# The differences of x on GpSimd instead of VectorE, with new places for every operation in a two-layer graph network

## The chip, the cores and the metric

The kernel runs on one core of one Trainium2 chip. A core has five engines that run side by side, each through its own queue in order: TensorE (PE, matrix products into PSUM), VectorE (DVE), ScalarE (ACT), GpSimd (POOL), and SyncE (SP), which here issues all the transfers. The metric is the device time of one execution in microseconds (us); the time of the kernel before is the median of three runs.

## The reference

The input is 64 independent graphs of 256 nodes, x of shape 64 x 256 x 256 (float32), and an adjacency matrix of integers for each graph. Two layers follow each other.

```
# layer 0, per graph: 8 heads of 32, four relations r, masks from the adjacency
q, k = x Wq + bq, x Wk + bk
attn = softmax(q k^T / sqrt(32))
out  = sum over r of (attn * (adj == r)) (x Wv[r] + bv[r])
x    = LN(x + out Wo + bo);  x = LN(x + gelu(x W1 + b1) W2 + b2)
# layer 1, per graph: two graph attentions, softmax over axis 1 (the columns' nodes)
for (W, a) in two layers:
    Wh = h W;  e = leaky_relu(Wh a1 + (Wh a2)^T)
    h  = softmax(where(adj > 0, e, -9e15), axis=1) Wh
x = LN(x + h);  x = LN(x + relu(x w_ff1 + b_ff1) w_ff2 + b_ff2)
```

Everything is float32. LN is a layer norm over the last axis.

## The kernel before

**One graph.** A graph is some 225 small operations, each a Python function that issues one or a few instructions for a whole graph (or a half or a head of it). Their short names are used throughout this text:

- load brings in x (xin, already cut into 32x32 squares) and the adjacency (adi). xT transposes x on VectorE. cast and jT make the transposed adjacency (adT) by a transfer. mask0 to mask3 compare it with the four relations, mask4 makes the mask of layer 1 (all on GpSimd).
- qk0 and qk1 are the products for q and k (half the heads each), qkc0 and qkc1 their copies out of PSUM. s0 and s1 are the scores. For each half m and each head h of it: max, exp, rec, nrm (the softmax; VectorE and ScalarE in turns), eT (transposition of the squares on VectorE), eW and eR (a write to HBM and a read from it, which finish the transposition), ec (a copy into PSUM on ScalarE), pm (three masks times the weights, VectorE), pl (the fourth mask, GpSimd). po0 and po1 are the products with the values, oT0 and oT1 their copies.
- The values of the four relations are computed with seven block products in place of eight, in the manner of Strassen and Winograd: vp1 to vp7 on TensorE. Four of them read differences of blocks of x, which xS (x_sums, L453) computes into the tile xs: t1 = a21 - a11, t2 = a22 - t1, t3 = a22 - a21, t4 = a12 - t2. The sums afterwards (va1 to va9 and the first copy vc1) put the values together; vb1 and vb0 add the bias on GpSimd.
- wo, ya: output product and residual. y and yb load and prepare the residual. st, rt, nb, ln with a number from 1 to 4: the four layer norms (VectorE, GpSimd, GpSimd, ScalarE); lg and lb: gain and shift on GpSimd.
- The two feed-forward parts have the prefixes a and b: T, W, R (transposition by way of HBM), u0 to u3 (products), x0 to x3 (activation, Gelu for a, Relu for b), S1 to S4 (differences on GpSimd for a second seven-product scheme), d1 to d7 (its products), e (sums out of PSUM), g and r (residual on GpSimd).
- Layer 1: hT, hW, hR (transposition), ga0, ga1, gac (first product and its copy), ip, z, zm, zx, ze, zd with A or B (masked softmax), h10 and h11, h1c (first attention and copy), h2, h2a (second attention, residual), store.

**The order.** There is no scheduler at run time. PLACES (L28 to L67) gives each operation a place in time, PERIOD is 60. Graph g's operation n stands at g x 60 + PLACES[n]; a sort over all graphs gives one list, and each engine's queue is that list cut down to its own operations (plan, near the end of the kernel). So in the steady part some six graphs are in work, each in another stage, and an instruction whose input is late holds up all that stands behind it on its engine. The values of the places are used for nothing but the order: the chip goes as fast as the waits allow. The loads of the weights (LOAD_PLACE, LOAD_STEP) and their preparation (V_PLACE, FFA_PLACE, GAT_PLACE, FFB_PLACE) are put into the same list.

**Buffers that tie the engines together.** All products but the scores and two banks of the feed-forward parts share two PSUM buffers (pool ps_mm, tag mm, two buffers). A product can start only when the product two before it in that pool has been copied or added out of PSUM. The copies pe of the attention weights share one PSUM buffer, so ec and pm take turns.

**Table loads.** ScalarE's functions come in sets. Between Exp and Gelu the compiler puts a table load ahead of the activation; the other functions used here need none. In the order before, the four Gelu activations ax0 to ax3 stand together between zeA and exp03, both Exp.

Of the kernel before, what the change touches and what calls it, by code (L numbers as in the profile page):

```python
# [14 lines left out]
ALU = mybir.AluOpType  # L15
# [10 lines left out]

PERIOD = 60.0
PLACES = {  # L28
    "load": 23.357, "xT": 44.608, "cast": 52.922, "jT": 64.605, "mask0": 69.219, "qk0": 72.09,
    "qkc0": 73.299, "mask1": 76.86, "s0": 78.011, "max02": 87.686, "exp02": 89.264, "qk1": 89.326,  # L30
    "max00": 91.141, "qkc1": 92.707, "exp00": 96.206, "rec02": 99.233, "max03": 99.873, "max01": 100.286,
    "mask2": 100.655, "rec00": 100.829, "nrm02": 101.294, "eT02": 101.781, "nrm00": 102.264, "xS": 102.642,
    "eT00": 102.765, "mask3": 102.981, "exp03": 104.45, "exp01": 105.68, "eW02": 108.309, "rec03": 109.52,
    "vp1": 110.158, "rec01": 110.803, "y": 111.209, "vc1": 113.257, "vp6": 114.571, "s1": 115.506,
    "va6": 115.853, "vp2": 116.039, "eR02": 119.674, "nrm01": 120.359, "max10": 120.437, "va1": 120.827,
    "yb": 121.298, "eW00": 123.019, "exp10": 123.155, "max11": 124.031, "nrm03": 124.245, "rec10": 125.086,
    "nrm10": 125.786, "max13": 129.917, "eR00": 129.963, "exp11": 130.688, "vp7": 131.698, "eT01": 131.873,
    "exp13": 132.201, "va7": 132.519, "vb1": 132.554, "eT10": 133.02, "max12": 133.458, "pl00": 133.78,
    "exp12": 134.344, "vp5": 135.541, "eT03": 136.074, "va9": 137.432, "va5": 137.492, "vp4": 138.406,
    "va4": 138.429, "eW03": 139.955, "ec02": 139.991, "eW01": 140.081, "pm02": 140.771, "eR01": 142.073,  # L40
    "rec12": 143.085, "pl02": 143.665, "rec11": 144.369, "rec13": 144.684, "vp3": 145.914, "ec01": 146.17,
    "nrm13": 147.545, "pm01": 149.231, "va3": 149.974, "nrm11": 150.098, "pl01": 150.355, "ec00": 151.68,
    "eR03": 151.833, "nrm12": 153.205, "mask4": 154.895, "eT13": 154.901, "pm00": 156.208, "ec03": 156.841,
    "vb0": 157.326, "eW10": 158.121, "pl03": 159.226, "eT11": 159.823, "pm03": 159.89, "eW13": 159.97,
    "eW11": 161.977, "po0": 162.822, "eR11": 162.889, "ec11": 163.67, "oT0": 164.697, "eR10": 165.613,
    "eR13": 166.702, "pm11": 167.743, "ec13": 167.832, "eT12": 167.88, "pl11": 170.085, "pm13": 170.45,
    "pl13": 172.693, "eW12": 172.935, "pl10": 173.109, "ec10": 174.083, "eR12": 178.038, "pm10": 178.658,
    "ec12": 179.982, "pm12": 181.436, "pl12": 183.147, "po1": 190.604, "oT1": 190.634, "wo": 195.515,
    "ya": 196.954, "st1": 198.358, "rt1": 200.264, "nb1": 202.568, "ln1": 205.212, "aT": 205.925,
    "aW": 214.402, "aR": 215.033, "au0": 217.723, "ag": 219.066, "ax0": 219.075, "au1": 220.077,  # L50
    "au2": 220.423, "ax1": 220.498, "au3": 221.942, "ax2": 222.429, "ax3": 223.227, "aS1": 224.059,
    "aS3": 226.672, "aS2": 228.949, "ad1": 229.288, "ad5": 232.772, "ad7": 233.221, "ar": 236.067,
    "ad6": 237.512, "aS4": 241.549, "ad2": 244.054, "ae5": 244.725, "ad3": 244.935, "ad4": 246.881,
    "ae1": 248.098, "ae6": 248.952, "ae": 249.383, "ae7": 250.355, "st2": 254.869, "rt2": 255.472,
    "nb2": 255.506, "ln2": 255.669, "lg2": 259.788, "lb2": 259.86, "hT": 261.844, "hW": 265.63,
    "hR": 271.783, "ga0": 272.609, "gac0": 274.207, "ga1": 274.252, "gac1": 274.962, "ipA": 275.589,
    "zA": 275.992, "zmA": 277.16, "zxA": 278.103, "zeA": 278.374, "zdA": 283.105, "h10": 283.502,
    "h11": 286.253, "h1c0": 287.71, "h1c1": 289.589, "ipB": 290.919, "zB": 291.939, "zmB": 292.107,
    "zxB": 294.725, "zeB": 295.859, "zdB": 298.561, "h2": 301.635, "h2a": 303.541, "st3": 304.449,
    "rt3": 304.465, "nb3": 307.95, "ln3": 307.966, "bT": 311.255, "bW": 313.954, "bR": 315.237,  # L60
    "bu0": 319.27, "bx0": 320.506, "bu1": 320.552, "bu2": 322.215, "bx1": 323.13, "bu3": 323.143,
    "bx2": 325.826, "bg": 326.199, "bx3": 327.872, "bd1": 328.16, "bS1": 328.916, "br": 329.424,
    "bd5": 330.387, "bS2": 331.057, "bS4": 331.173, "bS3": 331.831, "bd2": 334.692, "be5": 334.871,
    "bd3": 337.158, "bd4": 337.445, "bd6": 337.996, "be": 338.193, "be1": 338.799, "bd7": 340.197,
    "be6": 343.454, "be7": 346.517, "st4": 346.806, "rt4": 355.06, "nb4": 361.434, "ln4": 362.111,
    "lg4": 364.143, "lb4": 369.218, "store": 370.908,
}  # L67
LOAD_PLACE, LOAD_STEP = 62.0, 3.0
V_PLACE, FFA_PLACE, GAT_PLACE, FFB_PLACE = 92.0, 199.0, 202.0, 260.0

# [11 lines left out]
def kernel(  # L84
# [12 lines left out]
    nc = tc.nc  # L97
# [43 lines left out]
    def weight(w, name, mixed=False):  # L141

        k, n = w.shape[0] // P, w.shape[1]
        t = const.tile([P, k, n], F32, name=name)
        if mixed:
            mixed_rows(t, w)
        else:
            loads.append((t, w.rearrange("(k p) n -> p k n", p=P)))
        return t
# [13 lines left out]
    def rowvec(v, n, name):  # L163
        t = const.tile([P, n], F32, name=name)
        loads.append((t, _row(v, n)))
        return t
# [37 lines left out]
    wo, bo_r = weight(Wo, "wo"), rowvec(bo, D, "bo_r")  # L204
# [227 lines left out]
    class Graph:  # L432
# [15 lines left out]
        def x_sums(self):  # L448
            self.xs = fp.tile([P, 4, P], F32, tag="xs", name=f"xs{self.g}", bufs=1)
            (a11, a21), (a12, a22) = ([self.xT[:, k, c * P:(c + 1) * P] for c in range(C)] for k in range(KD))  # L450
            t1, t2, t3, t4 = (self.xs[:, i] for i in range(4))
            for o, t, u in ((t1, a21, a11), (t2, a22, t1), (t3, a22, a21), (t4, a12, t2)):
                nc.vector.tensor_tensor(o, t, u, ALU.subtract)  # L453

        def cast(self):
            self.adb = fp.tile([P, C, N], BF16, tag="adb", name=f"adb{self.g}", bufs=1)
# [355 lines left out]
```

## Time and profile before

| what | value |
|---|---|
| median of three runs | 3677.94 us (3675.18 to 3685.38) |
| the profiled execution, own time | 3687.13 us |
| its span | 3685.0 us |
| TensorE, busy | 3497.9 us |
| GpSimd, busy | 3019.8 us |
| VectorE, busy | 2880.7 us |
| ScalarE, busy | 2628.1 us |
| read from HBM and written to it | 243.42 and 201.33 MB |

The profile is one execution. The span runs from the first to the last instruction that it records. A row of instructions gives the line of the kernel, the engine, the operation, output and input tiles, their shapes and the count, then the busy time in us and the mean of one instruction in ns, then the engine's idle time just before them and what ended most of it. A row of a stretch of time gives its bounds and length, then for TensorE's matmuls, its weight loads, VectorE, ScalarE and GpSimd the busy time and in brackets the instructions, then the granted clock, the mean share of the transfer engines and GB/s. A row of waits gives the engine and the line that waited, what it waited for, the us in total, the number of times and the longest. A row of the chain of waits gives start and length in us, the engine, the tile and the line. A float32 matmul appears as two instructions.

### The profile page before, as it was taken

The page shows a single profiled execution, that of the slowest core. Times are in us where ns is not written, and L with a number is a line of the kernel's source. Part 1 is how long each engine was busy: PE and PEld are TensorE (multiplying, and loading weights), DVE is VectorE, ACT ScalarE, POOL GpSimd, SP SyncE. Part 2 cuts the span into 40 slices and gives each one's busy share as a digit, 9 for nine tenths or more (in the row PEclk, how much of TensorE's full clock was granted, in tenths as well). Part 3 has the DMA queues.
Part 4 walks back from the last instruction along what each step waited for, and adds up shares of the span by engine and source line. Part 5 has one row for each costly group of instructions (what it writes and reads, how often), then busy time and mean ns, then how long its engine had stood idle before and what let it go on. Part 6 is the DMA issues. An engine that isn't in the chain of part 4 may idle for free.

```text
span 3685.0 us, 73450 instructions
## 1 busy us (share of the span) xinstructions
PE 3497.9 (95%) x25816; PEld 2749.5 (75%) x25816; DVE 2880.7 (78%) x5208; ACT 2628.1 (71%) x6981; POOL 3019.8 (82%) x3142
## 2 busy tenths in 40 slices
PE   6799999999999999999999999999999999999995
PEld 3577777777777777777777777777777777777775
DVE  5688888878888888778788788788788888788762
ACT  4577777777777777777777777777777777777752
POOL 4588888888888888888888888888888888888864
PEclk8899999999999999999999999999999999999997
DMA  6344444444444444444444443444444444444420
GB/s 180 111 119 124 135 126 124 133 118 124 137 124 123 134 126 123 131 127 122 132 127 124 134 128 121 133 127 123 128 126 124 132 126 123 134 127 123 126 86 26
DMA packets 809889, 457.97 MB, mean 124 GB/s; under 512 B 334256, under 2 KB 718896, under 8 KB 809520
## 3 DMA queue, kind: packets, MB, share of 16 engines
q1 hardware_dynamic: 809520, 453.27, 42.1%
q8 instruction: 204, 3.34, 0.4%
q14 instruction: 165, 1.35, 0.1%
HBM read 243.42 MB, written 201.33 MB: 121 GB/s over the span
## 4 chain that ended last, share of the span: by engine, by line
PE 62%; DVE 17%; ACT 8%; DMA 6%; issue 3%; POOL 2%; SPq 2%; POOLq 0%; ACTq 0%; DVEq 0%
PE ffb_ps L387 10%; PE v_ps L511 9%; PE po L589 5%; PE ffa_po L422 5%; DVE pm L572 4%; PE ffb_pq L422 4%; PE qk_ps L487 4%; PE ffa_ps L387 4%; DVE eT_sq L306 4%; PE ffb_po L422 4%; PE ffa_pq L422 3%; PE ga_wps L619 3%; PE s L537 3%; DVE nmax L542 3%; PE h_ps L678 2%
## 5 line engine op out<-in xcount | busy, mean ns | idle before, releaser
L572 DVE TENSOR_TENSOR pm<-rel,pe 128x1536 f32<-128x1536 uint8 x512 | 891.4, 1741 | 123.4 <-ACT pe L568 110.7
L577 POOL TENSOR_TENSOR pl<-rell,eT 128x512 f32<-128x512 bf16 x512 | 595.9, 1170 | 15.5 <-DMA eT<-eT_d 15.2
L560 ACT ACTIVATE e<-e,rden 128x256 f32<-128x256 f32 x1024 | 463.0, 503 | 145.3 <-DVE rden L555 145.1
L387 PE MATMUL ffa_ps<-ffa_T,w 128*128 128x256 f32 x2048 | 478.2, 382 | 8.9 <-ACT e L550 3.3
L550 ACT ACTIVATE e<-s,nmax 128x256 f32<-128x256 f32 x1024 | 475.5, 475 | 5.6 <-DVE nmax L542 4.6
L387 PE MATMUL ffb_ps<-ffb_T,f 128*128 128x256 f32 x2048 | 458.0, 382 | 20.9 <-DMA ffb_T<-ffb_T_d 20.8
L387 PEld LDWEIGHTS ffb_ps<-ffb_T,f 128*128 128x128 f32 x2048 | 392.4, 192 | 102.9 <-issue 36.2
L387 PEld LDWEIGHTS ffa_ps<-ffa_T,w 128*128 128x128 f32 x2048 | 377.1, 192 | 55.3 <-ACT e L550 5.3
L589 PE MATMUL po<-pm,v 128*32 128x256 f32 x6144 | 363.7, 384 | 19.9 <-DVE pm L572 6.6
L568 ACT COPY pe<-eT 128x512 f32<-128x512 f32 x512 | 306.9, 599 | 87.0 <-ACT gb_wh L659 48.0
L306 DVE STREAM_TRANSPOSE eT_sq<-e 128x512 f32<-128x512 f32 x512 | 354.2, 692 | 14.9 <-DMA eT_d<-eT_sq 9.8
L542 DVE TENSOR_REDUCE nmax<-s 128x2 f32<-128x512 f32 x512 | 342.9, 670 | 5.8 <-PE s L537 5.8
L395 ACT ACTIVATE ffb_h<-ffb_ps,bf_c 128x256 f32<-128x256 f32 x512 | 212.4, 466 | 183.2 <-PE ffb_ps L387 183.2
L520 DVE TENSOR_TENSOR v<-v,v_ps 128x512 f32<-128x512 f32 x448 | 298.7, 678 | 35.0 <-PE v_ps L511 32.5
L430 DVE TENSOR_TENSOR ffb_res<-ffb_po,ffb_res 128x256 f32<-128x256 f32 (+2 forms) x256 | 130.4, 509 | 240.7 <-PE ffb_po L422 134.5
L589 PEld LDWEIGHTS po<-pm,v 128*32 128x32 f32 x6144 | 206.8, 110 | 149.1 <-issue 18.2
L479 POOL TENSOR_SCALAR rel<-adT 128x512 uint8<-128x512 bf16 x192 | 289.7, 1509 | 18.8 <-DMA adT<-adb 17.6
L528 POOL TENSOR_TENSOR v<-v,bv_r 128x512 f32<-128x512 f32 (+1 forms) x128 | 232.5, 1816 | 71.5 <-DVE v L520 71.5
L410 POOL TENSOR_TENSOR ffa_h<-ffa_h,ffa_h 128x512 f32<-128x512 f32 x64 | 82.0, 1281 | 221.9 <-ACT ffa_h L395 217.5
L395 ACT ACTIVATE ffa_h<-ffa_ps,b_c 128x256 f32<-128x256 f32 x512 | 212.2, 465 | 36.0 <-PE ffa_ps L387 35.0
L364 ACT ACTIVATE ffa_res<-ffa_res,nb_x,rs_x 128x256 f32<-128x256 f32 x256 | 139.9, 593 | 135.5 <-POOL nb_x L359 135.5
L550 ACT ACTIVATION_READ_ACCUMULATOR e<-s,nmax 128x1 f32 x1024 | 211.1, 206 | 0.0
(154 smaller groups left out, 8444.7 us busy)
## 6 DMA issues: line engine op xcount, KB each, us to landing
eT_d<-eT_sq SPq DMA_DIRECT2D x512, 256.0 KB, 3.1
eT<-eT_d SPq DMA_DIRECT2D x512, 256.0 KB, 3.1
xin<-in_x_dram SPq DMA_DIRECT2D x256, 64.0 KB, 2.7
adi<-in_adj_dram SPq DMA_DIRECT2D x64, 256.0 KB, 3.3
y<-in_x_dram SPq DMA_DIRECT2D x64, 256.0 KB, 4.6
ffa_T_d<-ffa_T_sq SPq DMA_DIRECT2D x64, 256.0 KB, 3.5
ffa_T<-ffa_T_d SPq DMA_DIRECT2D x64, 256.0 KB, 2.9
hT_d<-hT_sq SPq DMA_DIRECT2D x64, 256.0 KB, 3.2
```

Source lines behind the costliest of these rows:

```text
L306: nc.vector.transpose(self.sq.rearrange("p a c k y -> p (c k) a y"), src.rearrange("p c (k a x) -> p (c k) a x", k=KD, a=A))
L387: nc.tensor.matmul(p[:, f - f0, :], self.wa[:, k, f * P:(f + 1) * P], self.x.nodes(k), start=(k == 0), stop=(k == KD - 1))
L395: nc.scalar.activation(self.h[half][:, f1 + f, :], self.ps[f0][:, f, :], self.func, bias=self.ba[:, f0 + f:f0 + f + 1])
L422: nc.tensor.matmul(self.p[bank][:, k], a[:, f], seven[self.name[:3]][i][:, f], start=(f == 0), stop=(f == KF // 2 - 1))
L511: nc.tensor.matmul(self.ps["v", i], a, wv_s[i], start=True, stop=True)
L542: nc.vector.tensor_reduce(self.nmax[m, h], self.s4[m][h].rearrange("p (c n) -> p c n", c=C), AX.X, ALU.max, negate=True)
L550: nc.scalar.activation(e[:, ic, :], self.s4[m][h][:, ic * N:(ic + 1) * N], AF.Exp, bias=self.nmax[m, h][:, ic:ic + 1], accum_out=self.den[ ...
L560: nc.scalar.activation(e[:, ic, :], e[:, ic, :], AF.Copy, scale=self.rden[m, h][:, ic:ic + 1])
L568: nc.scalar.copy(self.pe[m, h], self.et[m, h].t.rearrange("p b c k y -> p (b c k y)"))
L572: nc.vector.tensor_tensor(self.pm[m, h], self.rel.rearrange("p r b c k y -> p r (b c k y)"), bc(self.pe[m, h], [P, R - 1, C * N]), ALU.mult)
L577: nc.gpsimd.tensor_tensor(self.pm_l[m, h], self.rel_l.rearrange("p b c k y -> p (b c k y)"), self.et[m, h].t.rearrange("p b c k y -> p (b ...
L589: nc.tensor.matmul(po[hp, :], self.v[m][:, jc, r, hp], w, start=(r == 0 and jc == 0), stop=(r == R - 1 and jc == C - 1))
```

## The change

The four differences of x_sums (L453) are issued by GpSimd instead of VectorE. All places are new: 225 of them and the five constants, so that the order on every engine's queue is another. PERIOD stays 60. The instructions themselves are otherwise the same, tile for tile.

```diff
@@ -26,47 +26,47 @@
 PERIOD = 60.0
 PLACES = {
...
-    "eT00": 102.765, "mask3": 102.981, "exp03": 104.45, "exp01": 105.68, "eW02": 108.309, "rec03": 109.52,
...
-    "vb0": 157.326, "eW10": 158.121, "pl03": 159.226, "eT11": 159.823, "pm03": 159.89, "eW13": 159.97,
-    "eW11": 161.977, "po0": 162.822, "eR11": 162.889, "ec11": 163.67, "oT0": 164.697, "eR10": 165.613,
...
-    "aW": 214.402, "aR": 215.033, "au0": 217.723, "ag": 219.066, "ax0": 219.075, "au1": 220.077,
-    "au2": 220.423, "ax1": 220.498, "au3": 221.942, "ax2": 222.429, "ax3": 223.227, "aS1": 224.059,
...
-    "zA": 275.992, "zmA": 277.16, "zxA": 278.103, "zeA": 278.374, "zdA": 283.105, "h10": 283.502,
-    "h11": 286.253, "h1c0": 287.71, "h1c1": 289.589, "ipB": 290.919, "zB": 291.939, "zmB": 292.107,
...
+    "qkc0": 97.949, "s0": 114.109, "mask1": 114.874, "max02": 120.516, "max01": 124.15, "exp02": 124.943,
...
+    "rec02": 126.88, "nrm02": 128.516, "max00": 137.875, "max03": 138.248, "exp01": 142.049, "xS": 142.083,
+    "eT02": 142.989, "exp00": 144.909, "rec01": 145.054, "qk1": 145.647, "exp03": 145.994, "eW02": 148.03,
...
+    "pl03": 192.932, "pl01": 194.193, "ec03": 194.796, "vb0": 194.872, "pm03": 195.848, "eT10": 196.442,
+    "eR13": 197.184, "eT12": 197.655, "po0": 199.032, "ec11": 199.429, "eW10": 200.338, "oT0": 203.052,
...
+    "aW": 243.237, "aR": 244.635, "au0": 248.422, "au1": 248.889, "ax0": 249.225, "ax1": 250.028,
+    "au2": 253.377, "aS1": 255.511, "ax2": 257.28, "au3": 257.297, "ag": 259.726, "ax3": 259.931,
...
+    "zA": 307.902, "zmA": 307.921, "zxA": 308.379, "zeA": 312.657, "zdA": 315.675, "h10": 324.462,
+    "h11": 325.343, "h1c0": 325.47, "h1c1": 325.478, "ipB": 327.18, "zB": 327.348, "zmB": 328.529,
...
-LOAD_PLACE, LOAD_STEP = 62.0, 3.0
-V_PLACE, FFA_PLACE, GAT_PLACE, FFB_PLACE = 92.0, 199.0, 202.0, 260.0
+LOAD_PLACE, LOAD_STEP = 96.0, 3.0
+V_PLACE, FFA_PLACE, GAT_PLACE, FFB_PLACE = 100.0, 240.0, 290.0, 300.0
@@ -450,7 +450,7 @@
             (a11, a21), (a12, a22) = ([self.xT[:, k, c * P:(c + 1) * P] for c in range(C)] for k in range(KD))
             t1, t2, t3, t4 = (self.xs[:, i] for i in range(4))
             for o, t, u in ((t1, a21, a11), (t2, a22, t1), (t3, a22, a21), (t4, a12, t2)):
-                nc.vector.tensor_tensor(o, t, u, ALU.subtract)
+                nc.gpsimd.tensor_tensor(o, t, u, ALU.subtract)
```

Two places are compared modulo 60, since the graphs follow each other at that distance. Counted from po0, the parts that the prediction speaks of stand like this in ScalarE's queue, around the end of a period:

```
before:  zA, exp00, ec03, zeA, ax0, ax1, nrm02, nrm00, ax2 | zdA, ax3, ec11, exp03, oT0, exp01, h1c0
after:   zA, nrm02, ax0, ax1, zeA, ec03, zdA, ax2 | ec11, ax3, exp01, oT0, exp00, h1c0
```

In the second line zeA, an Exp, stands between ax1 and ax2, both Gelu: the compiled program of the changed kernel has 255 table loads. In TensorE's queue the same stretch is, behind ga1 and ipA:

```
before:  d3, d4 (b), au0, d6, au1, d7, au2, au3 | po0, h10, h11, ad1, vp1, ipB
after:   au0, au1, d6, d2, d3, d4 (b), au2, au3, d7 | po0, h10, h11, qk1, ipB, ad1
```

GpSimd's queue has there, after: vb0, aS1, ag, xS, ar, aS3, aS2, aS4, pl11.

## The prediction

> **What bounds it now.** First the page's busy times, then the stretches of equal length, then TensorE's waits, then the chain of waits over one period.
>
> ```profile
> span 3685.0 us, 73450 instructions
> PE 3497.9 (95%) x25816; PEld 2749.5 (75%) x25816; DVE 2880.7 (78%) x5208; ACT 2628.1 (71%) x6981; POOL 3019.8 (82%) x3142
> ```
>
> ```profile
> 0.00:100.00 100.00, 57.60 (x318) 31.89 (x318) 55.97 (x94) 41.09 (x119) 42.45 (x41) 0.80 0.67 179
> ...
> 1000.00:2000.00 1000.00, 974.70 (x7275) 769.84 (x7274) 810.36 (x1466) 741.68 (x1974) 855.54 (x888) 1.00 0.43 127
> 2000.00:3000.00 1000.00, 974.85 (x7310) 768.88 (x7308) 809.92 (x1475) 741.09 (x1972) 849.74 (x884) 1.00 0.44 128
> ```
>
> In the middle TensorE is busy 97.5% at full clock and GpSimd 85%; the others have room. How long is one period (one graph)? The read of hT happens once per graph:
>
> ```profile
> L327 SPq DMA_DIRECT2D hT<-hT_d x36: 635/637/650, 1045.7 to 2978.8; - x36
> ```
>
> So 1933.1 / 35 = 55.23 us. TensorE's share is 0.9748 x 55.23 = 53.84 us, its idle time 1.39 us. Its waits between 1000 and 3000 us (36.2 periods) say where:
>
> ```profile
> PE h_ps L664 <- ACT oT L595: 31.2, 36, 1.4
> PE ga_wps L619 <- DMA hT<-hT_d: 10.1, 12, 2.7
> PE ffa_ps L387 <- DMA ffa_T<-ffa_T_d: 3.2, 4, 1.6
> ```
>
> Nearly all is one wait, 0.86 us per period, before the second half of h1: its PSUM buffer is released by ScalarE's copy oT0. The chain of waits shows why that copy is late:
>
> ```profile
> 1669.60 1.01 DVE xs L453
> 1671.33 0.62 DVE eT_sq L306
> ...
> 1672.45 0.50 ACT ga_wh L659
> 1672.94 0.72 ACT ffa_h L395 x2
> 1673.67 0.49 ACT pe L568
> 1674.17 1.28 ACT L550
> 1675.84 0.65 ACT e L550 x3
> 1676.80 1.14 PE h_ps L664 x4
> ```
>
> VectorE spends its time on xs ahead of the reciprocal for ScalarE's zdA (ga_wh); zdA holds up ax3 (ffa_h), ec11 (pe), a table load of 1.28 us (L550) and an exponential, and only then comes oT0. So xs is on the path that sets the period. 63 x 55.23 = 3479 us of the span are periods, 206 us are fill and drain.
>
> **What the Trainium skill says.** GPSIMD Engine Reference, section 8 (Key points): GpSimd shares its SBUF interfaces with VectorE, and contends with VectorE's instructions of two SBUF inputs. The trace agrees: the first of the four differences takes 247 to 1106 ns, the later ones 281 to 294 ns. ScalarE: Activation LUTs, What ACT_TABLE_LOAD costs: a load of about 1283 ns plus a drain of about 1380 ns. The trace has 1283 ns, and the activation starts at once behind it (load from 1663.95, next at 1665.25), so I use 1.28 us alone. Perfetto Trace Analysis, Identifying the Most-Contended Engine: matmul busy share is a poor measure of the distance to roofline. I therefore use it only for its complement, the idle gaps, which the waits confirm (1.28 of 1.39 us).
>
> **The change, part by part.**
>
> ```profile
> L453 DVE TENSOR_TENSOR xs<-xT 128x128 f32<-128x128 f32 x128 | 64.6, 505 | 0.0
> L453 DVE TENSOR_TENSOR xs<-xT,xs 128x128 f32<-128x128 f32 x128 | 36.9, 288 | 2.2
> ...
> L528 POOL TENSOR_TENSOR v<-v,bv_r 128x1024 f32<-128x1024 f32 x64 | 151.2, 2363 | 20.0 <-DVE v L520 20.0
> L528 POOL TENSOR_TENSOR v<-v,bv_r 128x512 f32<-128x512 f32 x64 | 81.3, 1270 | 51.5 <-DVE v L520 51.5
> ```
>
> Differences: VectorE loses (64.6 + 36.9) / 64 = 1.59 us per graph. GpSimd gets four of 128x128. The two L528 rows give (2363 - 1270) / 512 = 2.13 ns per column and 0.18 us fixed, so 0.45 us each, 1.8 us per graph (bounds: 1.3 us if the fixed part overlaps, 2.5 us if waits between the dependent ones show). GpSimd goes from 0.853 x 55.23 = 47.1 to 48.9 us of at least 53.84: still under TensorE. Its cover: the differences now stand right after ag, at about 52.5 us behind po0's start, and their first reader vp6 comes about 20 us later. What is behind them (ar, aS3, aS2, aS4, for the ad products) has about 5 us. If GpSimd were late by more than that, TensorE would pay one for one.
>
> Places: TensorE's 43 products per graph are the same, so its 53.84 us stay; only the idle time can move. I laid the new queues beside each other from po0's start, with the durations of the rows, and 0.25 us from a product's end to its reader (oT0 after po0 in the trace: 0.2 to 0.3). The tight places:
>
> h1's second half: after au2 ScalarE has a load 1.28, ax2 0.72, ec11 0.50, ax3 0.72, a load 1.28, exp01 0.92: 5.4 us. TensorE has au3 1.73, bd7 0.89, po0 3.59: 6.2 us. So oT0 starts when po0 ends, takes 0.27 to 0.37, and h10 (0.9 us) covers it, with 0.4 us left. The 0.86 us wait goes. Next late is the product behind h11, qk1, which needs h1c0 behind oT0 and exp00 (0.27 + 0.92 + 0.3 after po0 against 1.8 us of h10 and h11): about nothing left.
>
> Table loads: before, two per graph (L395 and L550). Now zeA (Exp) stands between ax1 and ax2 (Gelu), so there are four: +2.56 us for ScalarE, 0.742 x 55.23 = 41.0 to 43.5 us. One is between zA and ax0: zA, nrm02, load, ax0 end 3.9 us after au0's start; the reader bd2 comes at 1.73 + 1.73 + 0.89 = 4.35: 0.5 us left. The other, ahead of ax2, waits for au2: load and ax2 end 2.1 us behind it, po0 needs the buffer after 2.6 us: 0.5 us left. Without this cover each costs 1.28 us.
>
> Transfers: hT is issued behind lb2's transpose; 3.2 us to land, 3.8 us for the read (medians of the issues). It lands 1.2 us before ga0. For ffa_T, ya, st1, rt1, nb1, ln1 and aT (with GpSimd's lb2 and mask1 ahead of rt1) take 6.8 us from wo's end, the write 3.5, the read 2.9: 13.2 us and some issue time, against 13.6 us of products from wo's end to au0: 0.2 to 0.4 us left, about as before, where it stalled 0.09 us per period. SP passes the store between aW and aR, which is free while aW is in flight. The read eR11 now waits for pl01 at GpSimd's end of period, 1.8 us early for ec11.
>
> V products: vp5 needs va7, which reads vp7: 0.25 + 0.60 against vp2's 0.86, about 0.1 us short; wo after va1 about 0.1 us long.
>
> Sum per period: 0.1 (vp5) + 0.1 (qk1) + 0.2 (ffa_T) + 0.1 for the rest = 0.5 us idle in place of 1.39: period 54.3 us. 63 x 0.93 = 58 us less. Fill and drain: the same products in the same order until graph 2, the deferred loads at the same step, the GAT weights (L269 to L284, 14 us of TensorE and waits from 93.7 to 107.8) later; I take nothing, plus or minus 10 us. The profiled execution took 3687.13 us, 2.1 more than its span and 9.2 more than the median of 3677.94. So 3677.9 - 58 = 3620 us.
>
> **Rivals.** A: TensorE without gaps. The slacks above all hold, 0.1 us idle: 63 x 1.28 = 81 us less, 3597 us. For it: every queue but TensorE's has over 4 us free. Against: several slacks are near zero and transfers vary (the eT writes land in 2.0 to 6.0 us).
>
> B, slower: the table loads. If ScalarE comes to zA or to au2's end late by more than 0.5 us, the load is on TensorE's path, at bd2 and at po0. Both wholly exposed cost 2 x 1.28 us less nothing: idle 0.5 + 2.56 = 3.06 us, 63 x 1.67 = 105 us more, 3783 us; with the half-microsecond slacks still there 2 x 0.78 us, 2.06 us, 63 x 0.67 = 42 us more, 3720 us, which I take. It decides from 1.39 - 0.5 = 0.9 us of exposed load on. For it: ec00, just ahead of zA, waits for pm01 and for eR01's landing. Against: ec00 ends 0.2 us before the ips product.
>
> C, no difference: the wait on oT0 goes, but ffa_T or GpSimd's rt3 (which now stands behind mask0, held until pm12 is done) takes its place with 0.9 us: 1.4 us idle, 3678 us. For it: 0.3 us of slack on a path with two landings. Against: the same path stalled only four times in 36 periods.
>
> That the differences alone don't help is no case of its own: they are on the chain shown.
>
> **How the numbers follow.** Forecast 0.52 (own range 3600 to 3650), A 0.2, C 0.12 (3650 to 3690), B 0.16. Within 0.3% means 3667 to 3689, about what a measurement of this kernel tells from no change. Faster: forecast, A and a little of C, 0.74; same 0.10; slower 0.16. The range takes in A with a fill that is 12 us shorter (3585) and the lower half of B (3700); GpSimd's 1.3 to 2.5 us lies within its slack.
>
> **What would show it.** Right: h_ps waiting for oT near 0; 255 table loads (129 before) of 1283 ns; L453 on POOL at about 0.45 us; VectorE busy 2780, GpSimd 3130, ScalarE 2790 us; hT reads 54.3 us apart; TensorE over 98.5% in the middle. Wrong: pq waiting for ffa_h (L395), ffa_ps waiting for ffa_T in most periods, or any single TensorE wait over 0.9 us per period.

## The result, and the profile after

The changed kernel takes 3574.5 us (median of four runs, 3572.94 to 3575.81); the kernel before, beside it, 3680.6 us. The ratio is 0.9712, with a 95% interval from 0.9695 to 0.9729: 106 us less. The forecast was 3620 us, 58 us less. The direction and the mechanism were right, the size was not: the time fell below the low end of the range.

First the busy times of the changed kernel's page.

```profile
span 3571.2 us, 73514 instructions
PE 3477.1 (97%) x25816; PEld 2704.2 (76%) x25816; DVE 2805.2 (79%) x4952; ACT 2776.8 (78%) x7107; POOL 3117.9 (87%) x3398
```

VectorE, ScalarE and GpSimd stand at 2805, 2777 and 3118 us, where 2780, 2790 and 3130 had been worked out. The stretches of equal length (length, then busy time of TensorE's matmuls, its weight loads, VectorE, ScalarE, GpSimd) say more:

```profile
0.00:100.00 100.00, 59.55 (x332) 35.34 (x333) 59.37 (x96) 48.91 (x135) 47.23 (x51) 0.78 0.72 193
1000.00:2000.00 1000.00, 999.84 (x7493) 782.42 (x7486) 811.85 (x1431) 810.05 (x2075) 910.65 (x990) 1.00 0.45 131
```

In the middle TensorE has no idle time left: 999.84 of 1000 us, against 974.7 before. Its waits between 1000 and 3000 us, the whole list, are one line:

```profile
PE ffa_ps L387 <- DMA ffa_T<-ffa_T_d: 0.2, 1, 0.2
```

The wait for oT is gone, the waits for hT are gone, and nothing has taken their place. The hT reads, once per graph, give the period; first those between 1000 and 3000 us, then all.

```profile
L327 SPq DMA_DIRECT2D hT<-hT_d x38: 645/650/660, 1003.7 to 2987.5; - x38
L327 SPq DMA_DIRECT2D hT<-hT_d x64: 585/648/661, 141.6 to 3509.0; - x64
```

The period is (2987.5 - 1003.7) / 37 = 53.62 us, against 55.23: 1.61 us less. 63 periods give 101.4 us. The span fell by 3685.0 - 3571.2 = 113.8 us; the other 12.4 us are what is left over (fill and drain: span less 63 periods, 205.5 before and 193.1 after). The first hT read comes at 141.6 us in place of 161.2. The medians lie 106 us apart and not 114, because the profiled execution of before was 6.5 us above its median and that of after 1.6 us below.

The chain of waits of the changed kernel over the stretch where before it had run through xs, the table load and oT0 (start, length, engine, tile and line):

```profile
1663.08 3.46 PE ffa_ps L387 x16
...
1667.43 3.59 PE po L589 x64
1671.02 1.94 PE h_ps L664 x8
1672.96 0.73 PE qk_ps L487 x3
```

It is TensorE alone, one product after another: au2 and au3, bd7 (left out here), po0, h10 and h11, qk1. Over the whole execution it holds 95% of the chain. The moved differences and the table loads, by groups of instructions (busy time and mean, then the idle time before them):

```profile
L453 POOL TENSOR_TENSOR xs<-xT 128x128 f32<-128x128 f32 x128 | 59.2, 463 | 0.0
...
L395 ACT ACT_TABLE_LOAD x127 | 162.9, 1283 | 12.5 <-PE ffa_ps L387 12.2
L651 ACT ACT_TABLE_LOAD x65 | 83.4, 1283 | 3.6 <-DVE gb_max L646 2.5
```

The differences take 0.46 us each on GpSimd (the two with xs among their inputs 459 ns), 1.84 us per graph, as estimated (0.45 and 1.8).

### The profile page after: what moved, and what is told of

Its sections match the earlier page's. It is cut to its first block, busy times and chain, and to the rows that moved or that the text cites. A ratio compares the mean times of both kernels' runs of the same rounds, so it can differ in the third digit from the quotient of the medians.

```text
span 3571.2 us, 73514 instructions
## 1 busy us (share of the span) xinstructions
PE 3477.1 (97%) x25816; PEld 2704.2 (76%) x25816; DVE 2805.2 (79%) x4952; ACT 2776.8 (78%) x7107; POOL 3117.9 (87%) x3398
## 3 DMA queue, kind: packets, MB, share of 16 engines
q14 instruction: 167, 1.37, 0.1%
## 4 chain that ended last, share of the span: by engine, by line
PE 95%; DMA 1%; DVE 1%; SPq 1%; POOL 1%; ACT 0%; issue 0%; POOLq 0%; ACTq 0%; DVEq 0%
PE po L589 13%; PE ffa_ps L387 12%; PE ffb_ps L387 12%; PE v_ps L511 11%; PE qk_ps L487 6%; PE ffa_po L422 6%; PE ffb_po L422 6%; PE ffa_pq L422 5%; PE ffb_pq L422 5%; PE s L537 4%; PE h_ps L664 3%; PE h_ps L678 3%; PE ga_wps L619 3%; PE wo_ps L609 3%; SPq L139 1%; PE ga_ips L631 0%
## 5 line engine op out<-in xcount | busy, mean ns | idle before, releaser
L387 PE MATMUL ffa_ps<-ffa_T,w 128*128 128x256 f32 x2048 | 465.9, 381 | 8.3 <-DMA ffa_T<-ffa_T_d 8.2
L589 PE MATMUL po<-pm,v 128*32 128x256 f32 x6144 | 361.6, 384 | 15.7 <-POOL v L528 12.3
L395 ACT ACTIVATE ffb_h<-ffb_ps,bf_c 128x256 f32<-128x256 f32 x512 | 214.6, 470 | 160.6 <-PE ffb_ps L387 154.7
L589 PEld LDWEIGHTS po<-pm,v 128*32 128x32 f32 x6144 | 188.7, 110 | 184.1 <-ACT e L560 46.2
L395 ACT ACTIVATE ffa_h<-ffa_ps,b_c 128x256 f32<-128x256 f32 x512 | 208.5, 475 | 5.5 <-PE ffa_ps L387 3.8
L496 ACT ACTIVATE qT<-qk_ps,bqs_c 128x256 f32<-128x256 f32 x128 | 60.7, 474 | 188.5 <-PE qk_ps L487 188.5
L354 POOL TENSOR_TENSOR rs_x<-rs_x,nhalf 128x2 f32<-128x2 f32 x256 | 184.0, 719 | 21.3
L430 DVE TENSOR_TENSOR ffa_res<-ffa_po,ffa_res 128x256 f32<-128x256 f32 (+2 forms) x256 | 133.4, 521 | 69.9 <-PE ffa_po L422 65.6
```

The source lines that it names most:

```text
L387: nc.tensor.matmul(p[:, f - f0, :], self.wa[:, k, f * P:(f + 1) * P], self.x.nodes(k), start=(k == 0), stop=(k == KD - 1))
L395: nc.scalar.activation(self.h[half][:, f1 + f, :], self.ps[f0][:, f, :], self.func, bias=self.ba[:, f0 + f:f0 + f + 1])
L589: nc.tensor.matmul(po[hp, :], self.v[m][:, jc, r, hp], w, start=(r == 0 and jc == 0), stop=(r == R - 1 and jc == C - 1))
```

## The experiments

The runs stand in three groups, each with its own runs of the kernel before; ratios are compared, not times. In the first group before took 3686.1 us, in the second 3683.7 us, in the third 3684.0 us. Periods are worked out from the hT reads as above.

### One half of the change at a time

The differences alone on GpSimd, with the places of before:

```diff
--- kernel before
-                nc.vector.tensor_tensor(o, t, u, ALU.subtract)
+                nc.gpsimd.tensor_tensor(o, t, u, ALU.subtract)
```

> The kernel before with one line changed: the four differences on GpSimd, all places as before. Theory (VectorE's differences are on the path to oT0): 1.59 us leave VectorE ahead of the reciprocal for zdA, oT0 comes before h11 needs it, so the wait of h_ps on oT (0.86 us per period in the records, some 0.14 us more that the modelled ends hide) goes and the waits on hT and ffa_T stay: 63 x 1.0 = 63 us less, 3617 us (3600 to 3650), h_ps <- oT near 0. Rival (it is the new order that does it, the differences' engine does not matter): within 15 us of the kernel before, 3665 to 3680, h_ps <- oT still 0.8 us per period.

Measured: 3635.3 us, ratio 0.9864 (0.9849 to 0.9879), about 50 us less than before; period 54.34 us. From TensorE's waits of this kernel between 1000 and 3000 us, the largest and what is left of the wait for oT:

```profile
PE ga_wps L619 <- DMA hT<-hT_d: 6.2, 9, 1.8
...
PE h_ps L664 <- ACT oT L595: 0.7, 3, 0.4
```

The wait of h_ps for oT fell from 31.2 us to 0.7. So the reading of the chain before was right: xs on VectorE was what made oT0 late. Taking it away gave 55.23 - 54.34 = 0.89 us per period, about the 0.86 us of that wait. What it does not cure are the waits of ga0, for hT above all.

The places alone, with the differences back on VectorE:

```diff
--- changed kernel
-                nc.gpsimd.tensor_tensor(o, t, u, ALU.subtract)
+                nc.vector.tensor_tensor(o, t, u, ALU.subtract)
```

> The changed kernel with the differences back on VectorE, at the same new place (behind be7, ahead of eT02). Theory (the new places do nearly all by themselves, since VectorE has some 1.6 us to spare there: pm11, the next long one, waits for po0's end anyway): 3575 to 3590, TensorE still without waits. Rival (the differences must leave VectorE): 1 us idle per period comes back, 3620 to 3650.

Measured: 3585.7 us, ratio 0.9727 (0.9711 to 0.9743); period 53.81 us. The places alone bring nearly all of it, though on VectorE the differences now cost twice what they did before:

```profile
L453 DVE TENSOR_TENSOR xs<-xT,xs 128x128 f32<-128x128 f32 x128 | 104.8, 819 | 2.2
```

With the first and third, 102.5 us, that is 3.2 us per graph against 1.59, and TensorE hardly minds: the waits on record are 1.0 us in 2000. The two halves are therefore not two gains to be added (50 and 100 us, together 106): each takes the same wait away by itself, and the new places also take away the waits for hT and most of those for ffa_T. Which of the 225 places do it was tried for one alone, zeA (next experiment); for the others it stays open.

What the differences on GpSimd add to the new places is 0.19 us per period, 12 us by the periods and 6 to 8 us by the ratios (0.9727 against 0.9712 and, in the second group, 0.9706), whose intervals overlap. The trace shows where the 0.19 us lie. First TensorE's and then ScalarE's queue with the places alone, and last the same product (ad2, ffa_pq) in the changed kernel:

```profile
1682.08 1.95 PE L422 MATMUL ffa_po<-w,ffa_h 128*128 128x128 f32 x16
1683.95 1.16 PE L422 MATMUL ffa_pq<-w,ffa_h 128*128 128x128 f32 x8
```

```profile
1681.63 0.59 ACT L568 COPY pe<-eT 128x512 f32<-128x512 f32 x1 [1.01 <-DVE pm L572]
...
1683.06 0.83 ACT L638 ACTIVATE gb_z<-gb_ips,gb_wh 128x256 f32<-128x256 f32 x2
```

```profile
1676.61 1.06 PE L422 MATMUL ffa_pq<-w,ffa_h 128*128 128x128 f32 x8
```

In the changed kernel ad2 starts 0.16 us ahead of the recorded end of the product before it, as products in a row do. With the places alone the lead is 0.08 us, and ad2's first matmul takes 0.38 us in place of 0.28. That is so in each of the 37 periods between 1000 and 3000 us, and 0.08 + 0.10 us is about the difference. ad2 starts there 0.05 us after zB (gb_z) ends on ScalarE; in the changed kernel zB had ended 0.69 us before. ScalarE in turn had waited 1.01 us for VectorE's pm, which stands behind the slow differences. So the differences on VectorE still reach TensorE, by a stop too short to be listed as a wait.

### The two extra table loads

With zeA (Exp) put ahead of ax0 again there is no Exp between Gelus, and 129 loads instead of 255:

```diff
--- changed kernel
-    "zeA": 312.657,
+    "zeA": 309.0,
```

> The changed kernel with zeA moved ahead of ax0 in the order, so that there are two table loads per period instead of four (129 in all). Theory (the two extra loads are covered, and the price of having ax0 and ax1 early): ax0 now waits for zxA and zeA, ends about 1.2 us after bd2 wants its buffer, TensorE waits for it (ffb_pq <- ffa_h): 62 x 1.2 = 75 us more, 3650 us (3620 to 3670), though ScalarE is 2.56 us per period less busy. Rival (the loads cost something): 3574 or less.

Measured: 3678.4 us, ratio 0.9982 (0.9973 to 0.9991). With 126 table loads fewer, 2.5 us less work for ScalarE in every period, the kernel is some 100 us slower than the changed kernel, practically the kernel before. The theory had the direction and the place; its 75 us were too few. ScalarE's queue in this kernel (start, length, then in brackets the idle time ahead and what ended it), and below it TensorE's:

```profile
1646.20 0.51 ACT L651 ACTIVATE ga_z<-ga_z,ga_max 128x256 f32<-128x256 f32 x1 [0.85 <-DVE ga_max L646]
...
1647.31 1.28 ACT L395 ACT_TABLE_LOAD   x1
```

```profile
1646.97 1.05 PE L422 MATMUL ffb_po<-f_t,ffb_t 128*128 128x128 f32 x8
1649.50 1.16 PE L422 MATMUL ffb_pq<-f,ffb_h 128*128 128x128 f32 x8 [1.47 <-ACT ffa_h L395]
```

zeA needs the maximum from VectorE and waits 0.85 us for it; its own two exponentials with their accumulator reads take another 1.1 us; only then come the load and, at 1648.60, ax0, and bd2 waits for the buffer. The wait on record is 51.4 us in 36 periods, 1.43 us each, and the period is 55.31 us, 1.69 more than the changed kernel's. The two extra loads are the price for having zeA where nobody waits for it.

### How much slack ScalarE has at bd2

By the trace of the changed kernel, ScalarE's load and Gelus end about 0.4 us before bd2 needs their buffer:

```profile
1657.73 1.28 ACT L395 ACT_TABLE_LOAD   x1
1659.02 1.57 ACT L395 ACTIVATE ffa_h<-ffa_ps,b_c 128x256 f32<-128x256 f32 x4
...
1666.19 0.84 ACT L395 ACTIVATE ffa_h<-ffa_ps,b_c 128x256 f32<-128x256 f32 x2
```

```profile
1655.89 3.62 PE L387 MATMUL ffa_ps<-ffa_T,w 128*128 128x256 f32 x16
1659.35 1.05 PE L422 MATMUL ffb_po<-f_t,ffb_t 128*128 128x128 f32 x8
1660.24 1.06 PE L422 MATMUL ffb_pq<-f,ffb_h 128*128 128x128 f32 x8
...
1667.36 2.80 PE L589 MATMUL po<-pm,v 128*32 128x256 f32 x48
```

The four Gelu instructions of ax0 and ax1 run from 1659.02 to 1660.59; ax0 is the first two of them, and ends near 1659.85. bd2 starts at 1660.24, so 0.4 us are left. ax2 ends at 1667.03 and po0 starts at 1667.36: 0.3 us. To measure the first slack rather than read it, one or three extra copies of about 0.4 us were put just ahead of that load (range(1) below, and range(3)):

```diff
--- changed kernel, in Ffn.act
+                if f0 == 0 and self.func is AF.Gelu:
+                    for _ in range(1):
+                        nc.scalar.copy(self.h[0][:, 0, :], g1_r)
```

The changed kernel stood beside them:

> The changed kernel itself once more, as the mark for the other three of this group: the same ratio to the kernel before as measured first, 0.971, on a profile with hT reads 53.6 us apart and TensorE above 99.9% in the middle.

> The changed kernel with one more ScalarE copy of 128x256 (about 0.4 us) in each graph, just ahead of the table load of ax0; the copy's result is overwritten. Theory (the place beside bd2 has about 0.4 us of slack, as read from the trace): within 8 us of the changed kernel, TensorE waiting for ffa_h at L422 between 0 and 0.1 us per period. Rival (the slack is an artefact of modelled ends and in truth used up): 0.3 to 0.4 us per period, 19 to 25 us slower.

> As the kernel with one more copy, with three (about 1.2 us). Theory (0.4 us of slack, then one for one): 0.8 us per period, 50 us slower than the changed kernel, nearly all of it as TensorE waiting for ffa_h at L422. Rival (ScalarE's lateness is passed on to other places as well, as with the shortened table loads, where the recorded wait was 1.43 us but the period grew by 1.69): over 1.1 us per period, 70 us or more.

Measured: the changed kernel 3574.1 us, ratio 0.9706 (0.9691 to 0.972), period 53.62 us; one copy 3579.3 us, 0.9719 (0.9702 to 0.9735), period 53.68 us; three copies 3630.0 us, 0.9857 (0.9842 to 0.9872), period 54.52 us. So one copy costs 5 us, at the edge of what can be told (the intervals overlap), and three cost 56 us. By how much they make ScalarE late is best read from ax0: it starts 3.13 us behind au0 in the changed kernel, 3.44 with one copy, 4.31 with three (medians between 1000 and 3000 us). So ax0 is 0.31 and 1.18 us late, and the period 0.06 and 0.90 longer: 0.25 and 0.28 us were covered. The kernel with fewer loads gives a third point: ax0 5.09 us behind au0, 1.96 late, the period 1.69 longer, 0.27 covered. So the slack is 0.25 to 0.28 us, less than the 0.4 read from the trace, and behind it ScalarE's lateness goes one for one into TensorE. No wait is on record with one copy, but bd2's first matmul takes 0.36 us in place of 0.28 in 35 of 37 periods, and in none of the changed kernel's:

```profile
1662.77 1.14 PE L425 MATMUL ffb_pq<-f,ffb_h 128*128 128x128 f32 x8
```

So one copy just uses the slack up. With three copies the waits on record are at the place forecast (L425 and L398 are L422 and L395, three lines further down):

```profile
PE ffb_pq L425 <- ACT ffa_h L398: 25.5, 37, 0.7
```

### What stands right behind TensorE

Part of the computation left out, so that TensorE has less to do:

```diff
--- changed kernel, in the products of the feed-forward parts
-            for f in range(KF // 2):
+            last = KF // 2 - 1 if self.func is AF.Gelu else 1
+            for f in range(last + 1):
...
-                                 start=(f == 0), stop=(f == KF // 2 - 1))
+                                 start=(f == 0), stop=(f == last))
```

> The changed kernel with less TensorE work: each of the seven products of the second feed-forward part sums two of four blocks only, so half of that down product is left out. That takes 28 of its 56 block products, about 3.1 us of TensorE per period. Theory (TensorE alone sets the period): period near 50.5 us, some 195 us less than the changed kernel, 3380 us. Rival (GpSimd at 48.6 us per period, ScalarE's waits and the transfers stand right behind): period 51.5 to 52.5 us, 70 to 130 us less, with new waits of TensorE of 1 to 2 us per period.

Measured: 3506.5 us, ratio 0.9523 (0.9509 to 0.9537), 68 us less than the changed kernel; period 52.52 us. The theory fell. The rival comes close: its waits of 1 to 2 us are there, but the period and the gain lie just outside what it gave (51.5 to 52.5 us, 70 to 130 us). TensorE's largest waits of this kernel between 1000 and 3000 us:

```profile
PE po L590 <- ACT ffa_h L395: 44.9, 38, 1.2
PE ffb_pq L423 <- ACT ffa_h L395: 11.2, 37, 0.3
```

These are the two places with a table load, po0 and bd2, with 1.48 us per period between them. In this order of the queues TensorE leads the next bound by only 53.62 - 52.52 = 1.1 us per period. (The shortened products bd6 and bd7 stand right ahead of bd2 and po0 and are part of what covers the table loads, so this is a bound for this way of shortening TensorE's work, not for every one.)

### The fill

The five constants that place the weights' loads and preparation, set back to where they stood in the kernel before, counted from the new places:

```diff
--- changed kernel
-LOAD_PLACE, LOAD_STEP = 96.0, 3.0
-V_PLACE, FFA_PLACE, GAT_PLACE, FFB_PLACE = 100.0, 240.0, 290.0, 300.0
+LOAD_PLACE, LOAD_STEP = 98.2, 3.0
+V_PLACE, FFA_PLACE, GAT_PLACE, FFB_PLACE = 128.2, 235.2, 238.2, 296.2
```

> The changed kernel with the one-time work (the loads of the weights and the four preparations) put where it stood before, counted from po0: loads from 98.2, V at 128.2, first feed-forward at 235.2, attention weights at 238.2, second at 296.2. Theory (the fill became 20 us shorter because this work stands elsewhere): the first read of hT comes at about 160 us instead of 141.6, 3590 to 3597 us. Rival (the graphs' own new order shortened the fill): the first hT within 5 us of 141.6, 3570 to 3580 us.

Measured: 3580.3 us, ratio 0.9713 (0.9699 to 0.9728), by the ratio not to be told from the changed kernel. The first hT read is at 151.1 us, about half way back to 161.2, but the last one at 3515.1, 3 to 6 us after the changed kernel's (3509.0 and 3511.7 in its two profiles). So the constants account for half of the earlier first read, and most of that doesn't reach the end: neither the theory's 3590 to 3597 us nor the rival's first read came out.

Two tries for a shorter fill, with three constants, and with V_PLACE alone of them:

```diff
--- changed kernel
-LOAD_PLACE, LOAD_STEP = 96.0, 3.0
-V_PLACE, FFA_PLACE, GAT_PLACE, FFB_PLACE = 100.0, 240.0, 290.0, 300.0
+LOAD_PLACE, LOAD_STEP = 96.0, 4.0
+V_PLACE, FFA_PLACE, GAT_PLACE, FFB_PLACE = 139.0, 240.0, 290.0, 310.0
```

> The changed kernel with three constants of the start alone: LOAD_STEP 4.0, V_PLACE 139.0, FFB_PLACE 310.0, so that the weights' preparation stands later in the queues. Theory (the fill is set by waits for weights and by the v products' weights on VectorE, the largest of them po waiting for v, 12.3 us once): first hT read 3 to 8 us earlier than in the changed kernel (141.6 to 143.0 us), ratio to the kernel before 0.968 to 0.970. Rival (the waits at the start stand behind each other, so that one removed gives its time to the next): first hT within 2 us, same ratio, 0.9706.

> The changed kernel with V_PLACE 139.0 alone (the preparation of the v products' weights on VectorE stands behind the first maxima and reciprocals of graph 0). Theory: half of what the three constants give, first hT 1 to 4 us earlier. Rival: no change within 2 us.

Measured: 3575.0 us, ratio 0.9701 (0.9682 to 0.972), first hT at 141.8 us; and 3576.6 us, 0.9704 (0.9681 to 0.9726), first hT at 144.2 us. Both the same as the changed kernel: the rival's case. TensorE's waits in the first 400 us show why; of the kernel with three constants, the largest and one that is new there:

```profile
PE po L589 <- POOL v L528: 14.4, 1, 14.4
...
PE ga_wps L619 <- DMA hT<-hT_d: 6.1, 1, 6.1
```

The longest wait, 12.3 and 12.9 us in the changed kernel's two profiles, did not shrink (with V_PLACE alone it is 12.4), and a wait for hT came that was 0.9 us in the first of these. No run here that does the whole computation is faster than the changed kernel.

## Why the prediction was right and wrong

**The mechanism: right.** The wait of h10 and h11 for oT0 was set by xs on VectorE; with the differences alone moved it goes from 31.2 to 0.7 us. But they are not what most of the gain hangs on: the new places take the same wait away with xs still on VectorE. The signs named came true: 255 loads of 1283 ns, L453 at 0.46 us on GpSimd, the three other engines' busy times within 1% of their estimates, TensorE over 98.5%. Only the hT reads, foreseen 54.3 us apart, were closer.

**The table loads: right.** Two more per period cost nothing while covered. The slack at bd2 was put at 0.5 us; the trace shows 0.4 and the copies measure 0.25 to 0.28. At po0 0.5 was worked out, and the trace shows 0.3. So rival B's premise (lateness of ScalarE beyond a slack lands on TensorE) was right, with half a microsecond put too high, and its event didn't happen; the three copies and the kernel with fewer loads show what lateness at bd2 costs, 56 and 100 us.

**"Sum per period ... 0.5 us idle": this step failed.** Of 0.1 (vp5), 0.1 (qk1), 0.2 (ffa_T) and 0.1 for the rest, the trace shows 0.01 in all. (53.84 and 0.5 are 54.34; rounded to 54.3 this became 58 us in place of 56.) The largest term, ffa_T, was mis-sized because the durations of the transfers were taken over from before, 3.5 us for the write and 2.9 for the read. The issues of before between 1000 and 3000 us (KB each, median us from issue to landing), then of the changed kernel:

```profile
hT_d<-hT_sq SPq DMA_DIRECT2D x36, 256.0 KB, 3.2
...
ffa_T_d<-ffa_T_sq SPq DMA_DIRECT2D x36, 256.0 KB, 3.5
```

```profile
hT_d<-hT_sq SPq DMA_DIRECT2D x38, 256.0 KB, 2.1
...
ffa_T_d<-ffa_T_sq SPq DMA_DIRECT2D x38, 256.0 KB, 2.6
```

The same writes of the same size land 0.9 to 1.1 us sooner in the new order (those of eT too, 3.1 and 2.1), the read of ffa_T as before (2.9 and 2.9). In one period of the changed kernel, wo ends at about 1695.9, the write is issued at 1702.5, the read at 1705.1 and lands 3.0 us later, at 1708.1; au0 comes one period after 1655.89, at 1709.5. That leaves 1.4 us, not 0.2 to 0.4. The write's landing gives 0.9 of it; the rest is 0.2 on the way to aT, and issue time that had been allowed for.

It is the order that does this: with the differences alone moved, the writes of hT and ffa_T land in 3.3 and 3.5 us, with the places alone in 2.1 and 2.7. SyncE's queue around the write of ffa_T, before and after:

```profile
1652.85 0.64 SPq L327 DMA_DIRECT2D hT<-hT_d  x1
1653.59 1.17 SPq L315 DMA_DIRECT2D eT<-eT_d  x1
1654.85 0.45 SPq L311 DMA_DIRECT2D ffa_T_d<-ffa_T_sq  x1
```

```profile
1698.83 0.99 SPq L315 DMA_DIRECT2D eT<-eT_d  x2
1700.48 0.65 SPq L327 DMA_DIRECT2D hT<-hT_d  x1
1702.45 0.33 SPq L311 DMA_DIRECT2D ffa_T_d<-ffa_T_sq  x1
```

Both times the write is issued 2.0 us behind the read of hT. But before, a read of eT issued 1.2 us earlier still had 2.8 us to go; after, that read is 3.1 us old and has 0.3 us left (medians between 1000 and 3000 us). So the write before shared its time with one read more. That this is what made it slower fits both kernels, and the two with one half of the change as well; no run changes this one thing alone.

For vp5, the figures as written (0.25 + 0.60 against 0.86) leave nothing short, yet 0.1 was charged; it showed no idle time. For qk1, "about nothing left" was right to read and wrong to charge: the copy that it needs ends at 1672.73 and qk1 starts at 1672.80, and a slack of nearly zero costs nothing.

**"TensorE's share is 0.9748 x 55.23 = 53.84 us": 0.22 us too much.** This was taken for the floor, and rival A rested on it too. Busy share times period, both between 1000 and 3000 us:

| kernel | period | TensorE busy | product | recorded waits |
|---|---|---|---|---|
| before | 55.23 | 0.9748 | 53.84 | oT, hT |
| two loads | 55.31 | 0.9738 | 53.86 | bd2, each period |
| three copies | 54.52 | 0.9873 | 53.83 | bd2, each period |
| differences alone | 54.34 | 0.9908 | 53.84 | ga0, 15 waits in 37 periods |
| places alone | 53.81 | 0.9995 | 53.78 | hardly any |
| one copy | 53.68 | 0.9999 | 53.67 | none |
| after | 53.62 | 0.9999 | 53.61 | none |

TensorE's products are the same in all seven, yet those that stand still are "busy" for 0.2 us more. So a wait costs more than its record, and for the two kernels that wait at bd2 the traces show where. Products in a row start 0.16 us before the recorded end of the one ahead: in the changed kernel 1659.35 + 1.05 = 1660.40, and bd2 starts at 1660.24. With fewer loads the one ahead ends at 1646.97 + 1.05 = 1648.02 and bd2 starts at 1649.50. The record counts the time from 1648.02 on, but without the wait bd2 would have started 0.16 us before that; and its eight products then take 1.16 us in place of 1.06. Together that is 0.26 us beyond the record: 1.43 + 0.26 = 1.69, just what the period is longer by. With three copies 0.69 is recorded (25.5 / 37), 0.95 with these 0.26, and the period is 0.90 longer. A stop shorter than the 0.16 isn't on record at all: the places alone stop at ad2, and one copy at bd2. For the kernel before and the differences alone, whose waits stand elsewhere, this isn't worked out. The Trainium skill, Perfetto Trace Analysis, Tensor Engine Instruction, says that TensorE's recorded ends are estimated rather than observed, which fits ends that lie behind the next start. The prediction had cited that the matmul busy share is a poor measure of the distance to roofline, and had then used its complement as if that were exact.

**"Fill and drain ... nothing, plus or minus 10 us":** 12.4 us less between the two profiles, about 9 us when the second profile of the changed kernel is taken (3574.6 - 63 x 53.62 = 196.5, against 205.5), and some 5 us if the 101.4 us of the periods are taken from the 106 between the medians. Four to seven of the 9 to 12 go with the constants (200.4 with those of before); what gives the rest was not isolated.

Together: 63 x 0.46 = 29 us that had been charged for idle time (1.39 - 0.93), 63 x 0.22 = 14 us of idle time that the record calls busy, and 12 us outside the periods, are the 55 us by which 113.8 exceeds 58.

**The rivals.** A was the right case: the slacks all hold. Its 3597 us were too high by the 14 us of hidden idle time, by the 0.1 us per period (6 us) that it still charged, and by the fill. The low end of the range, 3585, had taken in A with a shorter fill; the hidden idle time and those 6 us took the result below it. C did not happen. GpSimd, at 91% in the middle, never held TensorE.

## What to carry to other kernels

When a kernel in a steady state has one engine that all others feed, price a new order by asking of each product whether its input is there, and charge nothing where the answer is "just in time": here such places, charged with 0.5 us in all, cost 0.01. Take the floor of TensorE from a stretch without waits, or expect it to lie a little under busy share times period when there are waits (0.26 us for each wait at bd2). And count table loads by where they stand, not by their number: here an order with 126 more of them, in places with 0.3 us of slack, is 100 us faster than one without, because they let an exponential stand where its input is ready.

## What had not been expected of the hardware

**Two inputs from SBUF on VectorE wait for GpSimd's whole instruction.** With the differences back on VectorE at the new places, VectorE's and then GpSimd's queue are:

```profile
1675.60 0.29 DVE L453 TENSOR_TENSOR xs<-xT,xs 128x128 f32<-128x128 f32 x1
1675.81 1.37 DVE L453 TENSOR_TENSOR xs<-xT 128x128 f32<-128x128 f32 x1
```

```profile
1675.61 1.43 POOL L410 TENSOR_TENSOR ffa_h<-ffa_h,ffa_h 128x512 f32<-128x512 f32 x1 [0.35 <-ACT ffa_h L395]
```

The same instruction takes 0.29 us, and 1.37 us when GpSimd has begun first: it ends at 1677.18, 0.14 us after GpSimd's at 1677.04. The next difference, from 1677.10, takes 1.37 us too, beside the GpSimd instructions that follow from 1676.99. The Trainium skill, SBUF — State Buffer, section "SBUF: two separate sides", calls this an exclusive lock held for the whole instruction, which the trace bears out. The transposition behind the differences, with one input, is not held up: 0.70 us beside GpSimd's next instruction, where its mean is 0.69. The prediction had read the long first difference in the kernel before as contention, but not that its length is what is left of GpSimd's instruction. There VectorE's and GpSimd's queue are:

```profile
1669.53 1.07 DVE L453 TENSOR_TENSOR xs<-xT 128x128 f32<-128x128 f32 x1
```

```profile
1669.15 1.30 POOL L410 TENSOR_TENSOR ffa_t<-ffa_h 128x512 f32<-128x512 f32 x1
```

GpSimd's ends at 1670.45, the difference at 1670.60, 0.15 us later.

**An order of queues changes the transfers' times.** The 256 KB writes of eT, hT and ffa_T went from between 3.1 and 3.5 us down to between 2.1 and 2.6 us with the same bytes per graph, while the mean rate in the middle rose from 127 to 131 GB/s, in step with the shorter period. Within the kernel before alone, between 1000 and 3000 us, the writes of eT sort themselves by how many other transfers are under way when they are issued: with none 2.0 us (median of 69), with one 2.9 (76), with two 3.3 (108), with three 4.5 (37). The write of hT always found loads of x and the adjacency under way before, and took 3.2 us; in the new order 36 of 38 find nothing, and it takes 2.1. The count is not all: in the changed kernel eT's writes with one other under way take 2.1 us (127). Of ffa_T's writes above, with two others under way before and after, the slower had more of one of them still to come. A forecast of a new order that takes the old durations of its transfers can be off by 1 us for each.
